# The transposed hidden columns of the last feed-forward leave PSUM in two copies of three slices

## The chip, the cores and the metric

The kernel runs on one core of one Trainium2 chip. The metric is the device time of one execution in microseconds (us); the time of a kernel is the median of its runs. The profile is a record of one execution, with its own time.

The core's engines that matter here are PE (TensorE, the matmuls), PEld (the weight loads of PE), DVE (VectorE), ACT (ScalarE), POOL (GpSimd) and SP, whose queue issues most DMAs. Each engine takes its instructions strictly in the order in which the program issued them.

## The reference

Two batches of 2048 tokens with 256 features go through an attention block and then a feed-forward whose products are taken with numbers rounded to FP4 by blocks of 16. Cut to what matters here:

```python
def fp4_linear(x, w):                       # both sides rounded by blocks of 16
    return jnp.einsum('bsk,nk->bsn', fp4_quant_dequant(x), fp4_quant_dequant(w))

gate = fp4_linear(x, w_gate)                # w_gate, w_up: (704, 256)
y = fp4_linear(x, w_up)
h = jax.nn.silu(gate) * y                   # 704 hidden columns
return fp4_linear(h, w_down)                # w_down: (256, 704)

x = x + ga * attention(norm(x))
x = x + gb * ffn(norm(x))
```

Before the last product the 704 hidden columns of a tile of 128 tokens must be rounded and then transposed, because the product runs over them and PE needs that dimension on the partitions.

## The kernel before

**Stages.** The attention of both batches takes most of the time; the feed-forward of batch 0 is spread out beneath the attention of batch 1. What is left at the end, with no attention to hide it, is the last feed-forward: batch 1, 16 tiles of 128 tokens (`t` = 0 to 15), each a chain `tail(b, t)`. This stage is called the tail below.

**One tile of the tail.** `tail_norm` normalizes and rounds the tokens (tile `w`). `tail` transposes them (`hq`), then multiplies by the gate weights into PSUM tile `pg` and by the up weights into `pu`, each in two halves of 352 columns. ACT takes the silu of `pg` into the first 704 columns of the SBUF tile `e` (line 1489), and DVE multiplies them with `pu` (1492). `quantize` (656) rounds them in place: a string of DVE instructions, one pass on ACT (with the operand `magic`, 702), and a last multiplication with the blocks' scales on POOL or DVE (711, 712). Then `transpose_hidden` (765) makes six transposes on PE, three into each of the two banks of one PSUM place (the tile `h2t`). One copy carries all six slices, 118 partitions by 768 columns, back into the last 768 columns of `e`. The projection `down` (1411) then adds six products over 117 or 118 partitions into the PSUM tile `dn` (line 1501). The profile counts two matmuls for each product in 32-bit floats: a projection shows as 12, a gate or up half (two products) as four; a transpose counts once. For `t` = 14 and 15 a product with an identity adds the residual into `dn` first; the other tiles add to the output in the DMA. `tail_out` (1506) copies `dn` to `y` and sends it out, by POOL's queue for the first 14 tiles and by SP's for the last two.

**The last tile** (`t` = 15) goes another way already, in `tail_part` (1532): it is cut in two parts of 352 columns, each with its own silu, rounding, three transposes, copy of 118 by 384 and three products.

**Rooms.** A chain takes rooms before it uses a buffer and gives them back after: three PSUM places `s` of two banks each (for `pg`, `pu`, `h2t`), two single banks `o` (for `hq`, `dn`), five tiles `e`. `h2t` also needs the single room `misc`; `OTHER` is one `s` and `misc`.

**Order.** The order on each engine is not written by hand: `Order.run` (180) plans it while the program is built. It keeps a clock for each engine with estimated costs, asks every active chain what it wants to issue next, and takes the instruction that can start first. Among those that can start within a short time of the first (`patience`, 0.12 us on PE, 0.05 on ACT, 0.04 on DVE) it takes the one with the earliest due time; an earlier tile is due earlier. A step follows its chain's last by `CROSS` = 0.2 us if it changes the engine; one in `Free` waits only for what the chain has waited for. Where a step is a `Best`, the planner chooses the engine by its estimated end: `copy` (425) prefers ACT by a margin of 0.5 us over DVE in the tail, and the last multiplication of `quantize` prefers POOL over DVE by 0.5 us. So a change of one chain's steps can change the order of the others.

Of the kernel before, what the change touches and what calls it, by code (L numbers as in the profile page):

```python
# [44 lines left out]
TAIL_MARGIN = 0.5  # L45
# [67 lines left out]
class Order:  # L113
# [23 lines left out]
    def signal(self, key, of=1, early=0.0):  # L137

        n, t = self.counts.get(key, (0, 0.0))
        n, t = n + 1, max(t, self.chain.end - early)  # L140
        self.counts[key] = (n, t)
        if n == of:
            self.done[key] = t
        return n == of

    def give(self, name, n=1, place=0):
        for _ in range(n):
            heapq.heappush(self.rooms[name], (self.chain.end, place))
# [190 lines left out]
def adaln_block(  # L339
# [32 lines left out]
    ROWS = -(-IH // 3)  # L372
# [8 lines left out]
        for n, e in (  # L381
# [7 lines left out]
    order = Order(  # L389
        rooms=dict(  # L390
            misc=MISC, s=3, o=2, e=5, head=2, osb=1, v=5, x=2, wv=1, wo=1,
            h=2, qm=2, h2=2, h2t=1, hqt=1, st=1, qs=3, ln=2,
        ),
        ahead=AHEAD,
        patience={"PE": PPE, "DVE": PDVE, "ACT": PACT},
    )
    signal, give, due = order.signal, order.give, order.due
# [14 lines left out]
    def banks(place, name):  # L412

        return ps_s.tile([P, 2, 512], F32, tag=f"s{place}", name=name)

    def leave(place):
        give("s", place=place)
        give("misc")

    OTHER = ["s", "misc"]  # L420

    def either(first, second, margin):
        return Best(first, second, margin=COPY_MARGIN if margin is None else margin)

    def copy(dst, src, margin=None):
        return either(A.copy(dst, src), V.tensor_copy(dst, src), margin)

    def matmuls(dst, pairs, first=True):
        return [
            T.matmul(dst, lhsT=l, rhs=r, start=(first and k == 0), stop=(k == len(pairs) - 1))  # L430
            for k, (l, r) in enumerate(pairs)
        ]
# [332 lines left out]
    def transpose_hidden(a, dst, name, margin=None):  # L765

        place, _ = yield Wait(take=OTHER)
        ps = banks(place, name)
        for i in range(2):
            op = transpose_half(ps[:, i], a, i)  # L770
            yield Free(op) if i else op
        yield copy(
            dst[0:ROWS].rearrange("p (i c) t -> p i c t", i=2),
            ps[0:ROWS, :, 0 : 3 * P].rearrange("p i (c t) -> p i c t", t=P),
            margin,
        )
        leave(place)

    def transpose_half(ps, a, i):

        return [
            T.transpose(
                ps[0:ROWS, c * P : (c + 1) * P],
                a[:, CHUNK_AT[3 * i + c] : CHUNK_AT[3 * i + c] + ROWS],
                ident,
            )
            for c in range(3)
        ]

    def half_of(ps):  # L790
        return ps[0:ROWS, 0 : 3 * P].rearrange("p (c t) -> p c t", t=P)
# [619 lines left out]
    def down(ps, h2t, wd, first=True):  # L1411
        return matmuls(ps[:, 0:D], down_pairs(h2t, wd), first)
# [4 lines left out]
    def residual(ps, b, t):  # L1417
        return T.matmul(ps[:, 0:D], lhsT=ident, rhs=x_tile(b, t), start=True, stop=False)
# [30 lines left out]
    def tail(b, t):  # L1449
        yield Wait([("normed", b, t)], ["o"])  # L1450
        order.step = max(order.step, order.chain.due)
        w, j, n = tails[b, t]
        ps = ps_o.tile([P, 512], F32, tag="o", name=f"hq{b}_{t}")
        yield [
            T.transpose(ps[:, k * P : (k + 1) * P], w[:, 0, j, k * P : (k + 1) * P], ident)
            for k in range(KC)
        ]
        yield copy(w[:, 1, j, :], ps[:, 0:D], TAIL_MARGIN if t > 1 else 0.0)
        give("o")
        _, *places = yield Wait(take=["e", "s", "s"])  # L1460
        e = spool.tile([P, N], F32, tag="e", name=f"e{b}_{t}")
        pg, pu = (banks(place, f"p{n}{b}_{t}") for n, place in zip("gu", places))

        split = t >= NT - SPLIT
        cols = [0, IH, I]
        parts = [(ps, wt, c) for ps, wt in ((pg, wg_t), (pu, wu_t)) for c in range(2)]
        if split:
            for c in range(2):
                order.add(tail_part(b, t, c, e, pg[:, c], pu[:, c], places), order.chain.due)
            parts = [parts[i] for i in (0, 2, 1, 3)]  # L1470
        for ps, wt, c in parts:
            yield Free(
                matmuls(
                    ps[:, c, 0 : cols[c + 1] - cols[c]],
                    [
                        (w[:, 1, j, k * P : (k + 1) * P], wt[:, k, cols[c] : cols[c + 1]])
                        for k in range(KC)
                    ],
                )
            )  # L1480
            signal(("up", b, t, ps is pu, c))
            signal(("up", b, t, ps is pu), of=2)
        if signal(("w used", b, t - j), of=n):
            give("v")
        if split:
            return
        h2 = e[:, 0:I].rearrange("p (c n) -> p c n", c=2)
        yield Wait([("up", b, t, False)])
        yield Free(A.activation(h2, pg[:, :, 0:IH], AF.Silu))
        give("s", place=places[0])  # L1490
        yield Wait([("up", b, t, True)])
        yield V.tensor_tensor(h2, pu[:, :, 0:IH], h2, ALU.mult)
        give("s", place=places[1])
        yield from quantize(e[:, 0:I], I // BLK, f"g{b}_{t}", e[:, I : 2 * I], TAIL_MARGIN)
        h2t = e[:, N - IC * P : N].rearrange("p (c t) -> p c t", t=P)
        yield from transpose_hidden(e, h2t, f"h2t{b}_{t}", TAIL_MARGIN)
        yield Wait(["wdb"], ["o"])
        ps = ps_o.tile([P, 512], F32, tag="o", name=f"dn{b}_{t}")
        if not added(t):
            yield Free(residual(ps, b, t))  # L1500
        for k, op in enumerate(down(ps, h2t, tails["w"], first=added(t))):
            yield Free(op) if k or not added(t) else op
        give("e")
        yield from tail_out(b, t, ps)

    def tail_out(b, t, ps):
        yield Wait(take=["h"])
        y = w2.tile([P, D], F32, tag="h", name=f"y{b}_{t}")
        yield copy(y, ps[:, 0:D], TAIL_MARGIN)
        give("o")  # L1510
        if added(t):
            yield Wait([("stored", b, t // 4)])
            yield G.dma_start(out[b, t * P : (t + 1) * P, :], y, accum_op=ALU.add)
        else:
            yield S.dma_start(out[b, t * P : (t + 1) * P, :], y)
        give("h")

    def added(t):

        return t < NT - BY_PRODUCT  # L1520
# [11 lines left out]
    def tail_part(b, t, i, e, pg, pu, places):  # L1532

        lo, n = i * IH, IH
        h2, m = e[:, lo : lo + n], e[:, I + lo : I + lo + n]
        h2t = e[:, N - (i + 1) * 3 * P : N - i * 3 * P].rearrange("p (c t) -> p c t", t=P)
        yield Wait([("up", b, t, False, i)])
        yield A.activation(h2, pg[:, 0:n], AF.Silu)
        yield Wait([("up", b, t, True, i)])
        yield V.tensor_tensor(h2, pu[:, 0:n], h2, ALU.mult)  # L1540
        if signal(("part", b, t), of=2):
            for place in places:
                give("s", place=place)
        yield from quantize(h2, n // BLK, f"g{b}_{t}_{i}", m, 0.0)
        place, _ = yield Wait(take=OTHER)
        ps = banks(place, f"h2t{b}_{t}_{i}")[:, 0, :]
        yield transpose_half(ps, e, i)
        yield copy(h2t[0:ROWS], half_of(ps), 0.0)
        leave(place)
        if i == 0:  # L1550
            yield Wait(["wdb"], ["o"])
            tails["o", b, t] = ps_o.tile([P, 512], F32, tag="o", name=f"dn{b}_{t}")
            yield Free(residual(tails["o", b, t], b, t))
        else:
            yield Wait([("down", b, t)])
        ps = tails["o", b, t]
        for c, r in enumerate(CHUNK[3 * i : 3 * i + 3]):
            yield T.matmul(
                ps[:, 0:D],
                lhsT=h2t[0:r, c, :],  # L1560
                rhs=tails["w"][0:r, 3 * i + c, :],
                start=False,
                stop=(i == 1 and c == 2),
            )
        signal(("down", b, t))
        if i == 1:
            give("e")
            yield from tail_out(b, t, ps)
# [132 lines left out]
```

## Time and profile before

| What | Value |
|---|---|
| runs of the kernel before | 1914.42, 1916.07, 1914.12 us; median 1914.42 |
| the profiled execution's own time | 1914.14 us |
| its span, first to last instruction | 1912.4 us |
| granted clock of PE, mean | 0.999 |
| busy share of the span: PE, DVE, ACT, POOL | 99%, 89%, 69%, 34% |
| first projection of the tail starts at | 1788.73 us |
| busy in 1780 to 1912.4 us (132.4 us): PE, DVE, ACT, POOL | 122.06, 119.46, 49.67, 28.48 us |
| copies of 118 x 768 in the tail | 15, all on ACT, about 0.80 us each |
| copies of 118 x 384 (both of tile 15) | 2, on ACT, 0.48 us each |

The busy shares are means over the whole span, which is attention for the most part; this change touches only the last 125 us or so. Times in the views count from the span's start. An entry such as "dn<-wdb,e x12" is a merged run of instructions on one engine, with the program's names of output and inputs, and a bracket behind it gives the idle time before it and what ended that. Every instruction is recorded at line 275, the planner's helper, so one goes by tile names.

### The profile page before, as it was taken

What the parts mean: (1) busy time and instruction counts of PE and PEld (TensorE: products, weight loads), DVE (VectorE), ACT (ScalarE), POOL (GpSimd) and SP (SyncE); (2) the same over time, 40 slices, a digit from 0 to 9 for tenths busy, and PEclk for the clock granted to TensorE, in tenths of its full rate; (3) what the DMA queues carried; (4) which work ended last, traced back from release to release, by engine and by line L of the source; (5) the groups of instructions that cost most, each with busy time, mean ns of one, the idle gap of its engine ahead of it and who ended that gap; (6) DMA issues with size and microseconds to landing.
All of it is one profiled execution on the core that took longest, in us unless ns stands there. A gap on an engine that the chain in (4) does not pass through costs nothing.

```text
span 1912.4 us, 30116 instructions
## 1 busy us (share of the span) xinstructions
PE 1886.6 (99%) x10184; PEld 782.2 (41%) x10184; DVE 1694.9 (89%) x3994; ACT 1326.6 (69%) x1463; POOL 648.6 (34%) x1419
## 2 busy tenths in 40 slices
PE   9999999999999999999999999999999999999998
PEld 5333333343333333343334443434434333335666
DVE  5999999999999998888898788798788988997997
ACT  4687677776776677766777667676676867786333
POOL 1343333333334332113445345454353212231221
PEclk9999999999999999999999999999999999999999
DMA  6422122112120223211112201210111111101011
GB/s 215 104 63 56 32 54 50 45 26 51 34 61 20 51 56 94 78 39 45 33 35 49 63 29 47 51 42 14 34 37 37 42 34 34 37 4 39 9 17 20
DMA packets 42249, 89.83 MB, mean 47 GB/s; under 512 B 6384, under 2 KB 24432, under 8 KB 38128
## 3 DMA queue, kind: packets, MB, share of 16 engines
q1 hardware_dynamic: 38720, 83.97, 17.0%
q0 software_dynamic: 2016, 1.84, 0.8%
q10 hardware_dynamic: 1360, 2.10, 0.3%
q8 instruction: 81, 1.33, 0.3%
q14 instruction: 72, 0.59, 0.1%
HBM read 63.51 MB, written 22.81 MB: 45 GB/s over the span
## 4 chain that ended last, share of the span: by engine, by line
PE 88%; DVE 9%; ACT 2%; issue 1%; POOL 1%; ACTq 0%; POOLq 0%
PE o L275 44%; PE ps L275 15%; PE v L275 6%; PE op L275 5%; DVE e L275 5%; PE dn L275 4%; PE qk L275 3%; PE up L275 2%; PE gate L275 2%; PE pg L275 2%; PE pu L275 1%; PE h2t L275 1%; ACT e L275 1%; PE busy L275 1%; DVE w L275 1%
## 5 line engine op out<-in xcount | busy, mean ns | idle before, releaser
L275 DVE TENSOR_SCALAR_CACHE_REDUCE e<-ps 128x1024 f32<-128x1024 f32 x1024 | 1227.3, 1215 | 102.0 <-PE ps L275 82.6
L275 ACT ACTIVATE e<-e,mn 128x2048 f32<-128x2048 f32 x512 | 1025.1, 2002 | 401.4 <-POOL mn L275 397.7
L275 PE MATMUL o<-e,vn 128*64 128x512 f32 x4096 | 992.7, 603 | 6.7 <-POOL vn L275 3.0
L275 PEld LDWEIGHTS o<-e,vn 128*64 128x64 f32 x4096 | 255.9, 136 | 454.5 <-issue 371.3
L275 POOL TENSOR_SCALAR mn<-mn 128x1 f32<-128x1 f32 x512 | 153.6, 300 | 689.2 <-DVE rz L275 315.1
L275 PE MATMUL ps<-q,k 64*128 64x512 f32 x2048 | 369.0, 444 | 2.0 <-DVE e L275 1.6
L275 PEld LDWEIGHTS ps<-q,k 64*128 64x128 f32 x2048 | 160.1, 184 | 345.3 <-DVE e L275 131.9
L275 POOL TENSOR_SCALAR vn<-v,rz 128x64 f32<-128x64 f32 x512 | 165.8, 324 | 295.3 <-DVE rz L275 207.4
L275 PE MATMUL op<-wo,osb 128*64 128x256 f32 (+1 forms) x960 | 125.6, 382 | 1.2 <-DVE x L275 1.0
L275 PE MATMUL v<-wv,ht 128*64 128x256 f32 x1024 | 124.5, 382 | 0.3 <-DVE e L275 0.3
L275 PEld LDWEIGHTS op<-wo,osb 128*64 128x64 f32 (+1 forms) x960 | 74.1, 140 | 60.4 <-issue 22.5
L275 PEld LDWEIGHTS v<-wv,ht 128*64 128x64 f32 x1024 | 71.1, 137 | 65.5 <-issue 26.3
L275 DVE RECIPROCAL rz<-z 128x1 f32<-128x1 f32 x512 | 80.3, 157 | 18.7 <-ACT e L275 17.8
L275 ACT ACTIVATION_READ_ACCUMULATOR e<-e,mn 128x1 f32 x512 | 95.5, 187 | 0.0
L275 DVE DVE_READ_ACCUMULATOR e<-ps 128x1 f32 x1024 | 84.4, 82 | 0.0
L275 ACT COPY osb<-o 64x512 f32<-64x512 f32 x108 | 62.4, 579 | 14.9 <-PE o L275 13.4
L275 PE MATMUL qk<-ht,wqk_sb 128*64 128x512 f32 (+1 forms) x224 | 61.8, 599 | 1.1 <-ACT ht L275 0.9
L275 POOL TENSOR_TENSOR h<-h,m 128x704 f32<-128x704 f32 x32 | 54.1, 1691 | 12.3 <-DVE m L275 5.4
L275 PE MATMUL dn<-wdb,e 117*128 117x256 f32 (+1 forms) x192 | 45.2, 383 | 5.0 <-ACT e L275 4.8
L275 DVE TENSOR_TENSOR x<-op,x 128x512 f32<-128x512 f32 (+1 forms) x59 | 39.7, 674 | 11.6 <-PE op L275 11.2
L275 ACT ACT_TABLE_LOAD x34 | 43.6, 1283 | 4.5 <-issue 3.9
L275 PE MATMUL dn<-wd_t,h2t 117*64 117x256 f32 (+1 forms) x384 | 46.0, 381 | 0.0
(249 smaller groups left out, 1449.0 us busy)
## 6 DMA issues: line engine op xcount, KB each, us to landing
k<-scr SPq DMA_DIRECT2D x124, 256.0 KB, 4.5
scr<-st SPq DMA_DIRECT2D x32, 512.0 KB, 3.1
q<-scr SPq DMA_DIRECT2D x124, 128.0 KB, 5.6
x<-in_x_dram SPq DMA_DIRECT2D x8, 512.0 KB, 4.2
wv<-in_wv_dram SPq DMA_DIRECT2D x8, 256.0 KB, 3.7
wo<-in_wo_dram SPq DMA_DIRECT2D x8, 256.0 KB, 2.7
xt<-in_x_dram SPq DMA_DIRECT2D x4, 512.0 KB, 7.9
out_dram<-h2t SPq DMA_DIRECT2D x16, 128.0 KB, 1.8
```

Of the source, the lines that this page charges most:

```text
L275: op = Op(self.name, *self.estimate(method, args, kw, lambda: f(*args, **kw)))
```

## The change

The tail no longer calls `transpose_hidden`. It issues the first three transposes, starts a new chain `second_half` with the same due time, and copies the first three slices. `second_half` issues the other three transposes into the other bank of the same PSUM place, copies slices 3 to 5, gives the place back and signals `transposed`. The projection's first three products follow the first copy; the fourth waits for `transposed`. Tiles 0 to 14 take this way; tile 15 and the feed-forward of batch 0 are as before.

```diff
-        yield from transpose_hidden(e, h2t, f"h2t{b}_{t}", TAIL_MARGIN)
+        place, _ = yield Wait(take=OTHER)
+        pt = banks(place, f"h2t{b}_{t}")
+        yield transpose_half(pt[:, 0], e, 0)
+        order.add(second_half(b, t, e, h2t, pt, place), order.chain.due)
+        yield copy(h2t[0:ROWS, 0:3, :], half_of(pt[:, 0]), TAIL_MARGIN)
         yield Wait(["wdb"], ["o"])
         ps = ps_o.tile([P, 512], F32, tag="o", name=f"dn{b}_{t}")
         if not added(t):
             yield Free(residual(ps, b, t))
         for k, op in enumerate(down(ps, h2t, tails["w"], first=added(t))):
-            yield Free(op) if k or not added(t) else op
+            if k == 3:
+                yield Wait([("transposed", b, t)])
+            yield Free(op) if k not in (0, 3) or k == 0 and not added(t) else op
         give("e")
         yield from tail_out(b, t, ps)
+
+    def second_half(b, t, e, h2t, ps, place):
+
+        order.chain.base = order.clock["PE"]
+        yield transpose_half(ps[:, 1], e, 1)
+        yield copy(h2t[0:ROWS, 3:6, :], half_of(ps[:, 1]), TAIL_MARGIN)
+        leave(place)
+        signal(("transposed", b, t))
```

## The prediction, made before the changed kernel ran

> **What bounds the kernel now.** I read first the page's shares, then busy time in stretches of 10 us over the tail, then the chain of work that ended last, then the timeline around each transposition. The shares (PE 99%) are those of the attention. The stretches say what the tail is like:
>
> ```profile
> 1840.00:1850.00 10.00, 8.87 (x36) 5.64 (x34) 9.97 (x22) 4.12 (x7) 1.40 (x2) 1.00 0.12 15
> 1850.00:1860.00 10.00, 9.89 (x44) 7.71 (x45) 9.90 (x29) 3.76 (x7) 2.52 (x3) 1.00 0.18 16
> 1860.00:1870.00 10.00, 8.76 (x38) 5.98 (x37) 9.97 (x21) 3.09 (x5) 1.38 (x1) 1.00 0.07 11
> 1870.00:1880.00 10.00, 9.70 (x45) 7.11 (x43) 8.79 (x24) 4.21 (x8) 1.74 (x2) 1.00 0.23 28
> 1880.00:1890.00 10.00, 10.00 (x45) 7.25 (x46) 8.38 (x21) 3.91 (x7) 2.25 (x2) 1.00 0.00 0
> ```
>
> The columns after the length are PE, PEld, DVE, ACT, POOL, the granted clock (1.00, so no clock effect), DMA. Up to 1870 DVE is full and PE is not; from 1870 to 1890 it is the other way round. Two engines share the bound. The chain that ended last goes through PE, with ACT at the changed place:
>
> ```profile
> 1866.71 0.67 PE h2t L275 x6
> ...
> 1867.46 0.81 ACT e L275
> 1868.27 0.04 issue
> 1868.31 2.86 PE dn L275 x12
> ```
>
> Six transposes, one copy of 0.8 us, then the projection: PE stands idle 0.94 us. In the timeline, of the 15 tiles concerned, four show this bare wait (projections at 1796.64, 1814.90, 1850.11 and 1868.31; idle 0.94, 0.89, 0.94, 0.94). At ten others a half or more of a gate or up product fills the gap and PE does not wait. The fifteenth, at 1901.07, has only the residual to fill it and waits 0.50. So the waits at stake come to 4.21 us, 0.22% of the time. How long the shorter form takes stands in the same trace, in the second part of tile 15:
>
> ```profile
> 1906.23 0.49 PE L275 MATMUL h2t<-ident,e 128*118 128x128 f32 x3
> 1906.80 0.48 ACT L275 COPY e<-h2t 118x384 f32<-118x384 f32 x1 [2.03 <-PE h2t L275]
> 1907.34 1.56 PE L275 MATMUL dn<-wdb,e 117*128 117x256 f32 x6 [0.61 <-ACT e L275]
> ```
>
> **PE, removed waits.** From first transpose to first product: 1.76 us now (1866.55 to 1868.31), 1.11 us with three slices (1906.23 to 1907.34). The other three transposes run within that time (six end 0.82 after the first starts), so a bare wait falls from 0.94 to 0.29: 0.65 saved, 0.60 at the one of 0.89. At 1901.07 the first product could start at 1899.32 + 1.11 = 1900.43, before the residual is through; ACT, which copies y from 1899.52 to 1899.89, is free just at 1899.32 + 0.57. All 0.50 goes. Sum: 3 x 0.65 + 0.60 + 0.50 = 3.05 us. The ten filled places give nothing.
>
> **The added wait.** The fourth product waits for the second copy. That starts behind the first, which starts 0.57 after the first transpose; two back-to-back copies of 256 columns at 1861.29 take 0.65 where one takes 0.37, an overlap of 0.09. So the second copy ends at 0.57 + 0.48 + 0.48 - 0.09 = 1.44, while three products need until 1.11 + 2.86 / 2 = 2.54. Cover 1.1 us: it costs nothing. If it were gone, behind the waiting product on PE stand the rest of dn, then the next tile's transposes and gate, and ACT's y copy. No DMA is added or moved; the output DMAs follow y as before.
>
> **ACT.** One copy of 0.798 becomes two of 0.478: 0.158 more in durations, 0.064 with the overlap, 15 x 0.064 = 0.96 us over the tail. ACT is busy 3.1 to 4.2 in 10, and this hides in its idle time; the pair starts 0.33 earlier (1906.80 - 1906.23 = 0.57 against 1867.46 - 1866.55 = 0.91) and so ends 0.27 earlier, which gives the PSUM place back sooner. Uncovered it could cost the whole 0.96. That is possible where ACT's next instruction is one that DVE needs:
>
> ```profile
> 1871.91 0.80 ACT L275 COPY e<-h2t 118x768 f32<-118x768 f32 x1 [0.33 <-PE h2t L275]
> 1872.61 0.72 ACT L275 ACTIVATE w<-w,magic 128x512 f32<-128x512 f32 x1
> ...
> 1873.36 0.69 DVE L275 SCALAR_TENSOR_TENSOR w<-w 128x512 f32<-128x512 f32 x1 [1.14 <-ACT w L275]
> ```
>
> DVE waits 1.14 us for a pass that stood behind y and the copy on ACT. Here the earlier end of the pair helps by 0.27, and a PE that is ahead helps more.
>
> The Trainium skill speaks against the change in "Perfetto Trace Analysis", section "Optimizing Scalar/DVE Operations": an instruction on ScalarE reading PSUM has a fixed overhead of some 51 ns, and grouping into larger ones pays where the engine is saturated. By the page the 15 extra copies would cost 0.77 us on ACT, against 0.96 by the rows. The same section says that breaking instructions up may let work finish sooner where the engine is not saturated but makes bubbles elsewhere; ACT at 3 to 4 in 10, with PE idle behind it, is that case by this trace.
>
> **How much of the 3.05 reaches the end.** Bounds: nothing, if DVE alone sets the end; 3.05, if all PE work moves up. Against nothing: the PE pieces from 1808 to 1892 follow each other on the chain with DVE nowhere on it. I looked at what each segment would hit on moving up. The transposes at 1848.35 need a PSUM place that DVE frees at 1847.05 by reading pu: 1.3 spare, 1.25 used by the two savings before. Those at 1866.55 have 2.3 spare, those at 1852.81, for POOL's multiplication, 2.0. Then DVE's waits:
>
> ```profile
> 1884.22 1.35 PE L275 MATMUL pu<-wu_t,w 128*128 128x352 f32 x4
> ...
> 1885.68 0.89 DVE L275 TENSOR_TENSOR e<-pu,e 128x704 f32<-128x704 f32 x1 [1.48 <-PE pu L275]
> ```
>
> With 2.55 saved by then, the 1.14 and most of the 1.48 go, so DVE moves up too, by up to 2.6 us. At the end DVE has finished tile 15 at 1904.72, and PE picks it up at 1906.23, 1.5 late; that margin and the DVE waits together exceed 3.05. So the full sum is possible with the order unchanged. But the planner orders anew: its own gap between last transpose and projection shrinks from 0.2 + 0.69 + 0.2 = 1.09 (estimate of the copy 0.05 + 768 / 1200) to 0.45. I take 2.0, two thirds, nearer the full sum because the chain is PE's and the spare times just suffice. Against the profiled execution: 1914.14 - 2.0 = 1912.14. The median of the runs lies 0.28 above that execution, so **1912.4**; its own range, with 3.05 and 0.5 saved, is 1911.4 to 1913.9.
>
> **Rivals.** (1) *DVE is the bound.* For it: 29.84 busy of 30 us up to 1870; it must do the same work after the change. Against it: its idle 1.14 + 1.48 later. Then only the 0.50 at the last projection counts: 1913.9. Chance 0.19.
>
> (2) *Slower: the projection jumps ahead of an up half that DVE waits for.* At 1830.80, 1884.22 and 1895.51 the filler between transposes and projection is half of pu. Now that the projection is ready 0.64 earlier by the plan, a filler that can start more than 0.33 after the transposes (0.45 less the patience of 0.12) goes behind it, since the older tile is due first. Each price is a projection, 2.6 us (1836.61 in the chain of waits), at the first two places, where DVE already waits 0.59 and 1.48; at the third DVE has 1.0 spare and 1.6 is left. Less the 2.0 saved: one place 1915.0, two 1917.6, all three 1919.2. It decides from the first place. Against it: these fillers now start at once behind the transposes. Chance 0.20, half of it with more than two places or like disorder on DVE.
>
> (3) *A better order.* Eight multiplications e<-e,s_g in the tail are on DVE, six on POOL; a chain ready earlier may find POOL the earlier end. Each that changes over takes 0.80 (1862.11 to 1862.91) off DVE; three with the 2.0 saved give 1914.4 - 4.4 = 1910.0. Against it: nothing says that they all go one way. Chance 0.12.
>
> (4) *It does not do what it says*: the product waits for both copies. Then 1.50 instead of 1.76, 4 x 0.26 + 0.26 = 1.3 saved: 1913.1. Against it: the first products of tile 15 at 1904.83 run before the second copy of the same tile e at 1906.80. Chance 0.04.
>
> **How the numbers follow.** Forecast 0.45, rivals 0.19, 0.20, 0.12, 0.04. Below 1910.2 lies most of (3), above 1917.0 half of (2): the range is 1910.2 to 1917.0. About 0.2% (3.8 us) is what a measurement of this kernel can tell from no change. Faster by more: 0.10 from (3) and 0.04 from the forecast's tail. Slower by more: 0.10 from (2). The rest, 0.76, is within.
>
> **What would show it.** In the profile after: 30 copies of 118x384 on ACT for tiles 0 to 14, none on DVE; projections about 1.1 us after the first transpose at bare places, with idle 0.3; no wait of PE inside a projection; DVE's waits near 1873 and 1885 shorter; last projection earlier by 2. Wrong if the sequence of gate, up and projection on PE differs, if DVE waits for pu longer than 1.5 us, or if POOL's share of the multiplications changes.

## The result, and the profile after

| What | Before | After |
|---|---|---|
| median, runs of the same comparison | 1915.32 us (15 runs) | 1918.45 us (15 runs) |
| range of these runs | 1914.12 to 1916.23 | 1917.7 to 1921.15 |
| span of the profiled execution | 1912.4 us | 1916.7 us |
| first transposes of hidden columns to the end of the span | 128.87 us | 132.07 us |
| sum of PE's idle waits in that stretch (number of stops) | 6.71 (12) | 8.84 (17) |
| sum of DVE's idle waits in that stretch | 4.27 | 6.91 |

The ratio is 1.0018, with a 95% interval of 1.0011 to 1.0025: slower by 3.1 us. The forecast was 1912.4, with a range up to 1917.0. The fourth row is the one to compare: it starts at the first `h2t` of the tail, and up to there both kernels issue the same work in the same order, so that what lies ahead of it (1.1 us in these two executions) is no effect of the change.

Busy time in stretches of 10 us over the tail, the changed kernel; after the length the columns are PE, PEld, DVE, ACT, POOL, the granted clock, DMA share and GB/s:

```profile
1840.00:1850.00 10.00, 9.70 (x41) 6.63 (x40) 9.96 (x26) 3.97 (x7) 2.20 (x2) 1.00 0.12 16
1850.00:1860.00 10.00, 9.38 (x44) 7.22 (x43) 9.32 (x26) 3.36 (x7) 2.25 (x2) 1.00 0.11 14
1860.00:1870.00 10.00, 9.71 (x37) 6.29 (x36) 8.60 (x19) 3.47 (x7) 2.01 (x2) 1.00 0.11 13
1870.00:1880.00 10.00, 8.75 (x43) 6.84 (x42) 9.93 (x25) 4.31 (x8) 1.91 (x2) 1.00 0.12 13
1880.00:1890.00 10.00, 9.09 (x40) 6.47 (x39) 8.84 (x20) 3.30 (x7) 2.27 (x2) 1.00 0.12 15
```

Before, DVE was full up to 1870 and PE from 1880 to 1890. Now PE has holes in every one of these stretches, and DVE in three of the five.

The first thing to look at is one bare place, tile 1 at the same position as before, in the chain of work that ended last of the changed kernel (start, length, engine and what):

```profile
1796.14 0.67 PE h2t L275 x6
...
1796.88 0.49 ACT e L275
1797.37 0.04 issue
1797.42 2.86 PE dn L275 x12
1800.28 0.66 PE h2t L275 x6
1800.94 1.19 PE pg L275 x4
1802.12 2.60 PE dn L275 x12
```

The copy is short, 0.49, but it starts behind all six transposes, not behind the third. In the timeline the first transpose starts at 1795.97, so the copy starts 0.91 after it, as the long one did; tile 15, whose two parts have a PSUM tile each and three transposes in it, has 0.57. In the changed kernel both banks belong to one PSUM tile. That this is why the copy waits for all six is shown below, by an experiment that gives the second three transposes a PSUM tile of their own. PE's wait at such a place falls from 0.94 to 0.62.

The chain shows a second thing. The bare projection takes 2.86 and the one with gate work in front of it 2.60. The same 0.26 stands between the two kinds of gate pieces in this chain, 2.63 after a wait and 2.37 without. So a stop of PE costs its wait and 0.26 more. The start times alone, which do not rest on modelled ends, say much the same: from the transposes' start to the next piece 1.45 with the wait and 0.65 without, from the projection's start to the next piece 2.70 and 2.60, so 0.90 for a stop with a wait of 0.62.

Then the order. Timeline of the changed kernel around tiles 9 and 10:

```profile
1867.33 2.53 PE L275 MATMUL pg<-wg_t,w 128*128 128x352 f32 x8
1869.70 2.53 PE L275 MATMUL pu<-wu_t,w 128*128 128x352 f32 x8
1872.06 0.82 PE L275 MATMUL h2t<-ident,e 128*118 128x128 f32 x6
1872.97 0.86 ACT L275 COPY e<-h2t 118x384 f32<-118x384 f32 x2 [2.26 <-PE h2t L275]
1873.50 2.86 PE L275 MATMUL dn<-wdb,e 117*128 117x256 f32 x12 [0.62 <-ACT e L275]
1876.21 0.82 PE L275 MATMUL h2t<-ident,e 128*118 128x128 f32 x6
1877.12 0.86 ACT L275 COPY e<-h2t 118x384 f32<-118x384 f32 x2 [0.34 <-PE h2t L275]
1877.65 2.86 PE L275 MATMUL dn<-wdb,e 117*128 117x256 f32 x12 [0.62 <-ACT e L275]
```

The planner put all of `pg` and `pu` of tile 13 ahead of the transposes of tile 9. Before, half of `pg` of tile 13 filled the gap of tile 10:

```profile
1871.01 0.82 PE L275 MATMUL h2t<-ident,e 128*118 128x128 f32 x6
1871.67 1.35 PE L275 MATMUL pg<-wg_t,w 128*128 128x352 f32 x4
1872.85 2.77 PE L275 MATMUL dn<-wdb,e 117*128 117x256 f32 x12
```

Now nothing is left for either gap. Over the tail, tiles 5, 10, 11 and 13 lose their filler (tile 11 keeps two transposes `hq`), tiles 1, 3, 7 and 9 stay bare, and there are eight bare places of 0.40 to 0.62 instead of four of 0.89 to 0.94. Further on, PE waits for DVE at tile 14, where before it did not:

```profile
1898.74 0.52 DVE L275 TENSOR_TENSOR e<-pu,e 128x352 f32<-128x352 f32 x1
...
1902.99 0.89 DVE L275 TENSOR_TENSOR e<-e,s_g 128x704 f32<-128x704 f32 x1
...
1903.93 0.87 PE L275 MATMUL h2t<-ident,e 128*118 128x128 f32 x6 [1.43 <-DVE e L275]
```

DVE multiplies `e` of tile 14 with `pu` at 1886.36 (1885.68 before), but its last multiplication for this tile comes at 1902.99, 6 us later than before (1896.86). The first line is a pass of tile 15 that DVE now takes before it has finished tile 14; before, it came behind (1897.90). So this wait comes with a new order on DVE.

The order on the other engines changed too. Of the multiplications with scales from 1780 us on, DVE has ten of 128 x 704 (nine before) and none of 128 x 512 (two before). At 1857.82 the projection of tile 8 went ahead of the second half of `pu` of tile 11, for which DVE then waited 1.36. That is the slower rival's mechanism, at another place.

### The profile page after: what moved, and what is told of

Its sections match the earlier page's. It is cut to its first block, busy times and chain, and to the rows that moved or that the text cites. A ratio compares the mean times of both kernels' runs of the same rounds, so it can differ in the third digit from the quotient of the medians.

```text
span 1916.7 us, 30128 instructions
## 1 busy us (share of the span) xinstructions
PE 1888.7 (99%) x10184; PEld 784.6 (41%) x10184; DVE 1695.3 (88%) x3993; ACT 1327.7 (69%) x1478; POOL 648.8 (34%) x1420
## 4 chain that ended last, share of the span: by engine, by line
PE 87%; DVE 9%; ACT 2%; issue 1%; POOL 0%; ACTq 0%; POOLq 0%
PE o L275 44%; PE ps L275 15%; DVE e L275 6%; PE v L275 6%; PE op L275 5%; PE dn L275 4%; PE qk L275 3%; PE up L275 2%; PE gate L275 2%; PE pg L275 2%; PE pu L275 2%; PE h2t L275 1%; ACT e L275 1%; PE busy L275 1%; DVE w L275 1%
```

## The experiments

Times are medians, and every ratio is to the kernel before in the same comparison, whose median lay between 1914.37 and 1914.96. In the changed kernel's own comparison it was 1915.32, so the tails are the safer measure for differences to its 1918.45. "Tail" is the time from the first `h2t` to the end of the profiled span, 128.87 before and 132.07 after.

**Copies and order taken apart.** The first kernel keeps before's plan and only issues its copy as two.

```diff
+        def halves_of(put):
+            for i in range(2):
+                put(dst[0:ROWS, 3 * i : 3 * i + 3, :], half_of(ps[:, i]))
+        op.ops[0].emit = lambda: halves_of(nc.scalar.copy)
```

> The order of the kernel before on PE, DVE and POOL, with each copy of 118 x 768 issued as two of 118 x 384 on ACT. Both halves are in one PSUM tile, so the first copy still waits for all six transposes, as in the changed kernel (first copy 0.91 us after the first transpose). Theory 1 (the new order costs the time, the two copies save a little): a bare wait of PE falls from 0.94 to 0.62, five places by 0.32, so 1.6 us less than before at most, 0.5 less at least. Theory 2 (the two copies themselves cost the time, through ACT and what stands behind them): slower than before by about 3 us.

1913.25 us, ratio 0.9991 (0.9982 to 1.0000), tail 127.08. The interval just reaches no change, but PE's waits fell by the expected 1.6, from 6.71 to 5.11. The reverse has the changed kernel's order with one copy of all six slices at the place of the first:

```diff
-        yield copy(h2t[0:ROWS, 0:3, :], half_of(pt[:, 0]), TAIL_MARGIN)
+        op = copy(h2t[0:ROWS, 0:3, :], half_of(pt[:, 0]), TAIL_MARGIN)
+        for o, put in zip(op.ops, (nc.scalar.copy, nc.vector.tensor_copy)):
+            o.emit = lambda put=put: put(
...
+            o.emit = lambda: None
```

> The order of the changed kernel on PE, DVE and POOL, but one copy of 118 x 768 in place of the two. Theory 1: slower than before by the changed kernel's 3.1 us plus 0.3 at some of its eight bare waits, so 3 to 5.5 us more than before. Theory 2: the two copies are gone, so within 1 us of before.

1921.51 us, ratio 1.0033 (1.0021 to 1.0046), tail 134.95. This is more than the 3 to 5.5 above the kernel before that were expected. So two copies save 1.5 us in the old order and 3.1 in the new one (1.8 and 2.9 by the tails), and the new order loses 5.2 to 6.7 (5.0 and 6.1 by the tails). That the copies themselves are the loss is out.

**The first copy freed from the last three transposes.** The second three go into a PSUM tile of their own, once in the old order and once in the new.

```diff
+            other.append(ps_o.tile([P, 512], F32, tag="o", name=name + "b"))
...
+                put(dst[0:ROWS, 3 * i : 3 * i + 3, :], half_of(other[0] if i else ps[:, 0]))
```

> As the first of these, and the second three transposes go to a PSUM tile of their own (one of the two single banks), so that the first copy waits for three transposes only. Theory 1: from first transpose to first product 1.11 us as in tile 15, bare waits 0.29; 1.5 to 3 us less than before. If DVE alone bounds the tail (rival 1 of the prediction): at most 0.5 us less. Theory 2: 3 us more than before, as in the first.

> The order of the changed kernel, and the second three transposes in a PSUM tile of their own. Theory 1 with the late first copy as a part of the loss: up to 8 x 0.33 = 2.6 us less than the changed kernel, so 0.5 to 3 us more than before; if the order alone makes the loss, because DVE is late in it, 2.5 to 3.5 us more than before. Theory 2: about 3 us more.

Old order: 1911.46 us, ratio 0.9982 (0.9973 to 0.9990), tail 125.41. New order: 1915.92, ratio 1.0005 (0.9996 to 1.0014), tail 129.57. Tile 1 in the old order, in the timeline:

```profile
1795.34 0.49 PE L275 MATMUL h2t<-ident,e 128*118 128x128 f32 x3
1795.66 0.49 PE L775 MATMUL h2t_1b<-ident,e 128*118 128x128 f32 x3
1795.92 0.48 ACT L792 COPY e<-h2t 118x384 f32<-118x384 f32 x1 [1.99 <-PE h2t L275]
1796.29 0.48 ACT L792 COPY e<-h2t_1b 118x384 f32<-118x384 f32 x1
1796.45 2.86 PE L275 MATMUL dn<-wdb,e 117*128 117x256 f32 x12 [0.30 <-ACT e L792]
```

The copy now starts 0.58 after the first transpose and PE waits 0.30, the forecast's figures. The gain of 3.3 in the old order is a little above the 1.5 to 3 expected. The early start is worth 1.8 us in the old order and 2.5 in the new.

**Only some tiles.** The split for five tiles at a time, one copy for the others, each with the plan that follows from it.

```diff
+        two = 0 <= t < 5
+        if two:
...
+        else:
+            yield from transpose_hidden(e, h2t, f"h2t{b}_{t}", TAIL_MARGIN)
```

> The change for tiles 0 to 4 only. PE's order differs from before in 6 rows, DVE's in 38. If the loss comes from orders in the first part of the tail: 1 to 4 us more than before. If it comes from the end alone (DVE takes work of tile 15 ahead of tile 14): within 1 us of before or less.

> The change for tiles 5 to 9 only. PE's order differs from before in 15 rows, DVE's in 72. If the loss comes from orders in the middle of the tail (a projection ahead of half of pu, passes of ACT behind copies): 1 to 4 us more than before. If it comes from the end alone: within 1 us of before or less.

> The change for tiles 10 to 14 only. PE's and POOL's order stay as before, DVE's differs in 5 rows. If new orders make the loss: no loss here, and one bare wait (tile 14) 0.3 us shorter, so 0 to 0.7 us less than before. If the loss comes from the end of the tail: 1 to 4 us more than before.

1915.58, 1916.26 and 1914.47 us; ratios 1.0005 (0.9997 to 1.0014), 1.0005 (0.9996 to 1.0014) and 0.9998 (0.9989 to 1.0007). None is told apart from the kernel before; the first misses the 1 to 4 us that new orders early in the tail were expected to cost. By the tails they are +0.64, +1.17 and -0.43, together +1.4 where the whole change has +3.2. The loss is not a sum over tiles, since each plan is made anew; no group of tiles holds it.

**DVE's waits taken away.** In the changed kernel DVE waits 1.77, 0.76 and 0.61 us for a pass of ACT that stands behind the copies. One run puts that pass ahead of the copies of tiles 4, 6 and 8, on ACT alone.

```diff
+    BEHIND = (4, 6, 8)
...
+        if t in BEHIND:
+            put = op.ops[0].emit
+            op.ops[0].emit = lambda: later.append(put)
```

> The changed kernel with one thing moved on ACT alone: the two copies of h2t for tiles 4, 6 and 8 stand behind the rounding pass of w (the one with the operand magic) instead of ahead of it. The order on PE, DVE and POOL is the changed kernel's. Theory 1a (DVE sets the end of the tail, and what the new order costs are DVE's waits for a pass that stands behind copies, 1.77, 0.76 and 0.61 us): these waits fall by some 2.5 us in sum and the time by 1.5 to 2.5 us against the changed kernel, although three projections start 0.7 us later. Theory 1b (PE sets the end, the new order costs by PE's eight bare waits): three projections 0.7 us later each, so the same time or up to 2 us more than the changed kernel.

1918.27 us, ratio 1.0016 (1.0007 to 1.0025), tail 132.12: no change. The first of these waits is 0.58 now, but DVE's wait for `pu` grew to 2.18, and PE's list of waits is the same within 0.01. DVE's waits were moved and not removed: their sum is 6.90 against 6.91. The other run takes the wait for `pu` away, by moving the projection of tile 8 behind the half of `pu` that it had overtaken, on PE alone (here and below, `held` keeps instructions back, and `then_held` issues them right behind the instruction that it is given):

```diff
+            if t == 11 and ps is pu and c == 1:
+                ops[-1].emit = then_held(ops[-1].emit)
...
+            if t == 8:
+                op.emit = lambda put=op.emit: held.append(put)
```

> The changed kernel with one exchange on PE alone: the projection of tile 8 is moved behind the second half of the up product of tile 11, so that DVE gets that half about 1.3 us earlier; the orders on DVE, ACT and POOL stay. Theory (DVE's wait of 1.36 at 1861.88 is carried on through DVE's list to PE's wait of 1.43 for e at the transposes of tile 14): the time falls by 1.0 to 1.4 against the changed kernel, to about 1917.2, some 2 above the kernel before; DVE's wait at that place is under 0.3 and PE's wait at tile 14 under 0.5. Rival (PE's own order and its bare waits set the pace, the wait of DVE is made up elsewhere): within 0.4 of the changed kernel.

1918.18 us, ratio 1.0018 (1.0009 to 1.0027), tail 132.15: the theory fell. Its timeline:

```profile
1855.96 2.53 PE L275 MATMUL pu<-wu_t,w 128*128 128x352 f32 x8
1858.33 2.76 PE L275 MATMUL dn<-wdb,e 117*128 117x256 f32 x12
1859.75 0.88 DVE L275 TENSOR_TENSOR e<-pu,e 128x704 f32<-128x704 f32 x1
...
1903.27 0.87 PE L275 MATMUL h2t<-ident,e 128*118 128x128 f32 x6 [1.44 <-DVE e L275]
```

DVE multiplies with `pu` without a wait, and 44 us later PE waits for DVE as long as ever. Most of what DVE gained it lost again waiting for later work of PE and ACT. So this wait of DVE costs nothing as long as PE's order stays. Why PE waits at tile 14 is not told by this run.

**The plan's own error.** The plan takes the first copy to start three transposes earlier than it does. One run tells it of the delay; two more leave the kernel before as it is and shift only the time at which the plan has its one copy end, by -0.1 and +0.2 us, to see what any small shift of the plan costs.

```diff
+        for o in op.ops:
+            o.delay = 3 * P / 1200
...
+        yield from transpose_hidden(e, h2t, f"h2t{b}_{t}", TAIL_MARGIN, -0.1)
```

> The change as it is, but the plan is told that the first copy ends 0.32 us later than it assumes, which is what the trace of the changed kernel shows (first copy 0.91 after the first transpose, where the plan has it three transposes earlier). PE's order then differs from before in 12 rows only. Theory (the new order is bad because the plan took the first copy to be early): at or below the kernel before, -1.5 to +0.5 against it. Rival (any order but that of before loses): +1 to +4 against it.

> The instructions of the kernel before, one copy; only the plan is told that the copy ends 0.1 us earlier than before, so that 15 rows of PE's order differ. Theory (the order of before is one good draw, and the plan's order gets worse with any small shift of its costs): +1 to +6 us against the kernel before. Rival (only the two copies lead the plan astray): within 1 us of the kernel before.

> The instructions of the kernel before, one copy; the plan is told that the copy ends 0.2 us later, so that 42 rows of PE's order differ. Theory (the order of before is one good draw): +1 to +6 us against the kernel before. Rival (only the two copies lead the plan astray): within 1 us of it.

1916.26 (ratio 1.0005, 0.9996 to 1.0014), 1915.83 (1.0004, 0.9996 to 1.0013) and 1916.25 us (1.0006, 0.9997 to 1.0015). The first misses its theory: by the tails its order loses 2.4 against the old one (129.51 - 127.08), not nothing, but half of the changed kernel's 5.0. The other two lie at the edge between their theories, +0.9 and +1.4, and the intervals hold no change. So a shifted plan may cost about 1 us here. Neither of these two came near 5 us; how far other shifts scatter was not tried. The plan's false start time of the copy has a part in the 5 us, about half by this run, and not the whole.

**PE's stops put in and taken out.** By now one account fitted every kernel but one (the split for tiles 5 to 9, 0.6 above) within 0.2 us: the tail is 118.9 us, plus PE's waits, plus 0.26 for each stop. Before: 128.87 - 6.71 - 12 x 0.26 = 119.04; after: 132.07 - 8.84 - 17 x 0.26 = 118.81; two copies in the old order, with 5.11 and 12 stops: 118.85. An account is no cause: PE has the same products and transposes to do in every kernel, so its busy and idle time must make up the tail, whatever brings the idle time about. So the next runs change the order on PE and nothing else. First, three stops are put into the old order: the transposes of tiles 5, 11 and 13 go behind the half of `pu` that filled the gap after them.

```diff
+            if t in (8, 14, 15) and ps is pu and c == 1:
+                then_held(ops[-1])
...
+            if moved:
+                put_off(op, None)
```

> Two copies in the old order, and on PE alone the transposes of tiles 5, 11 and 13 are put behind the half of the up product that filled the wait after them, as the changed kernel has them. Theory (PE sets the pace): three new stops of about 0.62 + 0.26, 2.6 us more than 1913.25: about 1915.9. Rival (the stops are made up elsewhere, and the loss of the new order comes from the orders on DVE, ACT and POOL): within 0.7 of 1913.25.

1915.86 us, ratio 1.0006 (0.9997 to 1.0015), tail 129.81: 2.6 us above the same kernel with its fillers, as the theory had it. Tile 5 in its timeline:

```profile
1829.37 2.53 PE L275 MATMUL pu<-wu_t,w 128*128 128x352 f32 x8
1831.74 0.82 PE L275 MATMUL h2t<-ident,e 128*118 128x128 f32 x6
1832.65 0.86 ACT L782 COPY e<-h2t 118x384 f32<-118x384 f32 x2 [2.32 <-PE h2t L275]
1833.18 2.86 PE L275 MATMUL dn<-wdb,e 117*128 117x256 f32 x12 [0.63 <-ACT e L782]
```

Then three are taken out of the changed kernel, and four out of the old order with two copies. The transposes go ahead of the half of `pu` that stood before them.

```diff
+            if t in (8, 13, 14) and ps is pu and c == 1:
+                put_off(ops, t)
...
+        if t in (5, 9, 11):
+            then_held(op[-1])
```

> The changed kernel, and on PE alone the transposes of tiles 5, 9 and 11 are put ahead of the second half of the up product that stands before them. Theory (PE sets the pace): waits of 0.62, 0.62 and 0.40 go, 1.64 + 3 x 0.26 = 2.4 us: about 1916.0 where the changed kernel has 1918.4. Rival (the orders on DVE, ACT and POOL are what loses): within 0.7 of the changed kernel.

> Two copies in the old order, and on PE alone the transposes of tiles 1, 3, 7 and 9 are put ahead of the second half of the up product that stood before them, so that this half fills the wait for the copy. Theory (PE sets the pace, and each stop of PE costs its wait and 0.26 for starting again): waits of 0.62, 0.57, 0.62 and 0.62 go, 2.43 + 4 x 0.26 = 3.5 us: about 1909.8 where the kernel with two copies in the old order had 1913.25. Rival (DVE, which now gets four up products 0.66 later, or the place in PSUM, sets the pace as soon as PE is ahead): less than 1 us of it arrives.

The changed kernel: 1916.61 us, ratio 1.0009 (1.0001 to 1.0018), tail 130.25, so 1.8 of the 2.4 expected; most of the missing part is a new stop of 0.15 + 0.26, where the transposes, moved forward, wait for DVE. The old order: 1910.17 us, ratio 0.9977 (0.9967 to 0.9986), tail 124.28, so 3.1 of 3.5 (2.8 by the tails), with one such stop as well. Its tile 1 in the timeline:

```profile
1793.10 1.35 PE L275 MATMUL pu<-wu_t,w 128*128 128x352 f32 x4
1794.29 0.82 PE L275 MATMUL h2t<-ident,e 128*118 128x128 f32 x6
1794.94 1.35 PE L275 MATMUL pu<-wu_t,w 128*128 128x352 f32 x4
1795.20 0.86 ACT L782 COPY e<-h2t 118x384 f32<-118x384 f32 x2 [1.14 <-PE h2t L275]
1796.13 2.76 PE L275 MATMUL dn<-wdb,e 117*128 117x256 f32 x12
```

No wait before the projection, and the copies end while PE still works on `pu`.

**How far it goes, and whether the split matters then.** The same four fillers in the version with the second PSUM tile, and in the kernel before with its one copy:

> The fastest so far (two copies in the old order, second three transposes in a PSUM tile of their own, 1911.46) with the transposes of tiles 1, 3, 7 and 9 ahead of the second half of the up product. Theory (PE sets the pace): waits of 0.30, 0.24, 0.30 and 0.29 and 4 x 0.26 go, 2.2 us: about 1909.3. Rival (DVE takes over as the bound, or the place in PSUM is late): 1910.8 or more.

> The kernel before with its one copy, and on PE alone the transposes of tiles 1, 3, 7 and 9 ahead of the second half of the up product. Theory (a stop of PE costs its wait and 0.26; a half of 1.18 hides the copy's 0.94 as well as a shorter one): waits of 0.94, 0.89, 0.94 and 0.94 go, 3.71 + 4 x 0.26 = 4.75, less a new wait for DVE of about 0.4 as in the run with two copies: about 1910.6 against 1914.9, so that the split is worth 0.5 or less once the places are filled. Rival (the split is worth its 1.5 in any order): 1911.7 or more.

1909.98 us, ratio 0.9974 (0.9964 to 0.9985), tail 123.98, and 1910.89 us, ratio 0.9981 (0.9972 to 0.9990), tail 124.65. The first missed its theory: 1.5 of 2.2 arrived. The second came to its theory's time, but its kernel before was faster in that comparison, so that it gained 3.5 where some 4.3 were expected (4.2 by the tails). The chain of the work that ended last says why; here is a stretch of it, of two copies in the old order with the fillers:

```profile
1804.14 1.60 DVE e L275 x2
1805.74 0.11 DVE q_g L275
1805.85 0.40 DVE w L275
1806.25 2.04 DVE e L275 x3
1808.29 0.11 DVE s_g L275
1808.40 1.19 DVE w L275 x3
```

From 1784 to 1895 us its chain has 81 us of DVE and 26 of PE; before it had 97 of PE and 1 of DVE. The chains of the two others go the same way, with 79 and 66 of DVE. With PE's stops gone, DVE, idle for 0.5 to 0.9 us only, sets the end. All three filled versions, at 1909.98 to 1910.89 us, beat the kernels before and after. What the split is worth once the gaps are filled stays open: 0.4 to 0.7 us by the tails, 1.3 and 1.5 by the differences from the kernel before in each comparison, with intervals that overlap.

## Why the prediction was wrong

**What bounds the kernel.** That the chain is PE's was right, and over most of the tail more so than I wrote: "Two engines share the bound" gave DVE a part that it takes over only once PE's stops are gone.

**Removed waits.** The step that failed first is "a bare wait falls from 0.94 to 0.29". It was read from tile 15, where the three slices have a PSUM tile of their own; here the first copy waits for all six transposes, and the wait falls to 0.62. Each place gains 0.32, and the last projection keeps 0.18 of its 0.50: five places give 1.6. The kernel with two copies in the old order measured 1.5. With the dependency gone it measured 3.3 against the forecast's sum of 3.05, and that sum had left out the 0.26 for the one stop that vanishes altogether. So the working was right for a copy that starts as assumed.

**The added wait and ACT.** Both prices held: no projection waits for its second copy, and the pair takes 0.86, as worked out. The times did not: the pair starts 0.91 after the first transpose, as the one copy did, so it ends 0.06 later than that and not 0.27 earlier, and the PSUM place comes back no sooner. The Trainium skill, "Perfetto Trace Analysis", section "Optimizing Scalar/DVE Operations", has some 51 ns for the extra instruction; the rows give 0.86 - 0.80 = 0.06. Its other sentence, that breaking instructions up may let work finish sooner where the engine is not saturated but causes bubbles elsewhere, agrees with -1.5 and -3.1 us at a fixed order.

**What reaches the end.** "I take 2.0, two thirds" failed, and with it the forecast. It rested on "the full sum is possible with the order unchanged", and the order did not stay. I had seen that the planner orders anew and took one third off for it; the new order costs some 5 us, about three times what two copies save in the old one. The prediction had named a new sequence on PE as a sign that it is wrong, and that sign came. The new order's price by the account, against two copies in the old order, is four new bare places (0.62 + 0.62 + 0.40 + 0.61 = 2.25, and 4 x 0.26 = 1.04) and the new wait of 1.43 + 0.26 at tile 14: 4.98 of the 4.99 between the tails. The bare places are shown by putting such stops in and taking them out. The wait at tile 14 stayed at 1.43 or 1.44 in every run that kept this order's end with two copies; no run took it away, so its part, a third of the 5 us, is argued only. The times of tiles 14 and 15 above point to DVE's new order as its cause, and no run put that order back.

**The rivals.** The slower rival had the sign but not the cause. A projection did jump ahead of an up half that DVE waits for, and undoing that changed nothing. The cause of the larger part, 3.3 of the 5.0, is what I did not list: transposes that the planner leaves until after their filler. The shift of multiplications (rival 3) happened in both directions. Putting stops into PE's order, with the lists of DVE, ACT and POOL untouched, moved the time by the stops' price, so that part needs no shift; no run took the new lists of DVE, ACT and POOL with the old order on PE, so a part of theirs in the rest is not ruled out. Rival 4 was half true: not the product but the first copy waits for everything.

**Left open.** What tile 14's wait costs by itself was not measured. Why the planner's clocks put the transposes so late was not followed step by step.

## What to carry to other kernels

When a planner or a list scheduler orders the work, a change of one step is two changes; measure the step in the old order and the new order with the old step before either is believed. On an engine that paces a stage, count its stops: here each cost its wait and 0.26 us, and issuing the transposes ahead of independent matmuls saved more (three places in the old order are worth 2.6 us, four 3.1) than a shorter copy behind it (1.5). Before a short copy is taken to start early, look at what it waits for: two halves of one PSUM tile waited for the writers of both, and the copy started 0.34 us later at each place.

## What the runs showed of the hardware

PE's start after a stop costs 0.26 us beyond the wait: pieces of 2.86 against 2.60 and 2.63 against 2.37 in the chain. The ends of matmuls are modelled in these records, but start times alone give about the same, and with this term the account gives 118.8 to 119.1 for the tails of 16 of the 19 kernels; the other three, two of them bound by DVE, come to 119.2, 119.5 and 119.6. The Trainium skill, "TensorE: Matmul & The Clock Gate", section "Single matmul latency", has a constant of 398 cycles at 2.4 GHz in the latency of a single bf16 matmul, by estimate 0.17 us. That is a latency and not the price of a stop; what the traces here show for a stop, with 32-bit floats, is larger, and no run takes such a matmul alone.
